# In-place quantization, seven tiles of x, and an order rule for chain matmuls in layer 0 of a two-layer transformer kernel

## The chip, the cores and the metric

The kernel runs on one core of one Trainium2 chip. The metric is the device time of one launch in microseconds (us), as the median of several executions. A core has five instruction queues that run side by side, each in its own order: TensorE (PE, matmuls, with the weight loads PEld beside them), VectorE (DVE), ScalarE (ACT), GpSimd (POOL) and SyncE (SP, which here only issues DMAs). An instruction that waits holds up everything behind it in its queue.

## What is computed

The input x is 16 sequences of 512 tokens, 128 wide. Two layers follow each other; the change touches only the first:

```
x = x + 0.5 * ffn0(layernorm(x))      # half-step feed-forward, I = 352
x = x + attn0(layernorm(x))           # 16 heads of 8, relative positions in a band of +-64
x = x + 0.5 * ffn0(layernorm(x))      # the same feed-forward again

def fp4_linear(x, w):                 # ffn0: gate, up and down are all of this form
    # both sides: blocks of 16 values, scale = max|x|/6, round to the grid 0 .5 1 1.5 2 3 4 6
    return einsum(quant(x), quant(w))
score = q.k + q.rel_emb_k[dist];  attn = softmax(score)
ctx   = attn.v + attn.rel_emb_v[dist]
```

Layer 1 (linear attention and a mixture of experts, each in half-steps) reads the result from DRAM. Its code is not changed.

## The kernel before, in words

Layer 0 is a software pipeline over 32 units: 16 sequences `b`, two halves `h` of 256 tokens each, unit `u = 2b+h`. A unit passes these steps, written as Python generators that yield after each small step:

- **head** and **tail** (`F.half`, L107 to L140): the first and the second feed-forward of a half. Layer norm (`ln_steps`, L48 to L63), quantization (`quant_steps`, L64 to L82), transposes of the quantized x (L115), gate and up matmuls (L121, L125) with the activation between (ACT L122, DVE L123, L126), quantization of `h`, transposes (L133), two ACT copies (L135, L136), down matmuls (L139), and the sum into x on DVE (L140). This is a chain: each link is a few tenths of a us on another engine. `quant_steps` runs on DVE (L70 to L78) and ends in two POOL instructions (L79, L81); it writes the scaled values into a tile `q_y` of its own.
- **prep**, **prepV**: the projections to q, k and v, written to DRAM as f16 pairs and read back in the layout of the scores (`BD`, `TQ`, `KS`).
- **maxima** (L333 to L356): all 32 score tiles of a unit are computed on PE (`scores`, L255 to L267: four matmuls L263, eight more L267 where the tile lies in the band), and DVE takes the maxima of each (L341, at high priority). Then DVE reduces them (`mk`, L347), PE transposes the result (L349), and the negative maximum goes by DRAM into a row of `BD`. I call these scores X.
- **main** (L358 to L415): the same 32 score tiles again, now with the maximum subtracted; ACT writes the exponentials (L369) into `PT`. I call these scores M. Both kinds take turns in one PSUM pool `sps` of three tiles. After every eight M scores a run of 16 matmuls averages v (`av`, L272 and L274); for the relative values there are band runs (`rps`) of 16 or 32 matmuls, copied by ACT (L403). At the end the band part goes through DRAM (`RD`, then `cr`).
- **fin** (L417 to L444): DVE adds the two parts (`cx`, L422), PE transposes (L430), DVE divides (L433, L434), PE transposes again (L437), ACT copies (L438), PE multiplies with the output weights (L440), and DVE adds into x (L443).

`interleave` (L446) sets the order in which these generators emit. Each has a number of steps and a start and an end in units; the generator whose next step is due first goes next. A main has 59 steps in its unit (32 scores, four empty steps after each average, and others), the stream of maxima 33 per unit, fin starts 1.45 units after its main started. Tiles of x come from a pool of five; `xload(b)` is called in the first step of head(b).

The emitted order is not the issued order. A list scheduler with a timeline of its own sorts the instructions of each engine by priority and by when it believes them ready, so a chain matmul may stand in PE's queue before a score that was emitted earlier. `tc.issue_after(i)` adds an edge that only fixes the issue order on i's engine; it waits for nothing. `run` (L270) already uses it to keep a run together.

Of the kernel before, what the change touches and what calls it, by code (L numbers as in the profile page):

```python
# [8 lines left out]
F32 = mybir.dt.float32  # L9
# [16 lines left out]
class K:  # L26
# [23 lines left out]
    def ln_steps(s, xb, out, wk, n):  # L50
# [12 lines left out]
        yield  # L63
    def quant_steps(s, X, wk, P, nb, tag):  # L64

# [7 lines left out]
        y=wk.tile([128,max(704,n)],F32,name=("q_y","q_yw")[n>704])[:,:n]; y3=y.rearrange("p (b k) -> p b k",k=16)  # L73
# [10 lines left out]
class FFN:  # L84
# [22 lines left out]
    def half(f, xb, half, wk, pp):  # L107
# [3 lines left out]
        xn=wk.tile([128,2,128],F32,name="f_x")  # L111
# [3 lines left out]
        for j in range(2): nc.tensor.transpose(ps[:,j*128:(j+1)*128],xq[:,j*128:(j+1)*128],s.ident)  # L115
        xqT=wk.tile([128,256],F32,name="f_x"); nc.scalar.copy(xqT,ps[:,:256]); yield
        h=wk.tile([128,2,I],F32,name="f_h")
        for j in range(2):
            t=h[:,j,:]
            g=pp.tile([128,512],F32,name="mps")  # L120
            nc.tensor.matmul(g[:,:I],xqT[:,j*128:(j+1)*128],f.wguT[:,0,:],start=True,stop=True)  # L121
            nc.scalar.activation(t,g[:,:I],AF.Tanh,scale=0.5)  # L122
            nc.vector.scalar_tensor_tensor(t,t,1.0,g[:,:I],ALU.add,ALU.mult); yield  # L123
            u=pp.tile([128,512],F32,name="mps")
            nc.tensor.matmul(u[:,:I],xqT[:,j*128:(j+1)*128],f.wguT[:,1,:],start=True,stop=True)  # L125
            nc.vector.scalar_tensor_tensor(t,u[:,:I],0.5,t,ALU.mult,ALU.mult); yield  # L126
        for hq in s.quant_steps(h.rearrange("p a b -> p (a b)"),wk,128,44,"hq"): yield
        hq=hq.rearrange("p (a b) -> p a b",a=2)
        for j in range(2):
            ps=pp.tile([128,512],F32,name="mps")  # L130
            for c in range(3):
                P=min(128,I-c*128)
                nc.tensor.transpose(ps[:P,c*128:(c+1)*128],hq[:,j,c*128:c*128+P],s.ident)  # L133
            hT=wk.tile([128,3,128],F32,name="hT",bufs=1)
            nc.scalar.copy(hT[:,0:2,:],ps[:,:256])  # L135
            nc.scalar.copy(hT[:96,2,:],ps[:96,256:384])  # L136
            for c in range(3):
                P=min(128,I-c*128)
                nc.tensor.matmul(ps[:,384:512],hT[:P,c,:],f.wdT[:P,c,:],start=(c==0),stop=(c==2),skip_group_check=True)  # L139
# [6 lines left out]
class Attn0:  # L146
# [110 lines left out]
    def scores(a, out, kt, half, b, BD, TQ, KS):  # L257
# [4 lines left out]
        for g in range(4):  # L262
            nc.tensor.matmul(o4[:,g],KS[:,sd,g*512+kt*128:g*512+(kt+1)*128],BD[:,g,:,b*32:b*32+32].rearrange("p h (x j) -> p x h j",j=4),start=(g==0),stop=(not ib and g==3),skip_group_check=True)  # L263
        if ib:
            for x in range(8):
                w0=kt*128-blk*32-x+a.OFF
                nc.tensor.matmul(out[:,x*64:x*64+64],a.ET[:,w0:w0+128],TQ[:,:,b*32+4*x:b*32+4*x+4],start=False,stop=(x==7),skip_group_check=True)  # L267

    xnT={}; pend={}; last=None
# [5 lines left out]
    def prep(a, b, xb, wk, pM):  # L275
# [6 lines left out]
        for j in range(4): nc.tensor.transpose(ps[:,j*128:(j+1)*128],xn[:,j,:],a.ident)  # L282
        xnT=a.xnT[b]=wk.tile([128,512],F32,name="xnT",bufs=2); nc.scalar.copy(xnT,ps); yield
        for z in range(2):
            ps=pM.tile([128,512],F32,name="mps")
            nc.tensor.matmul(ps,a.w[:,z*128:(z+1)*128],xnT,start=True,stop=True)
# [18 lines left out]
        nc.tensor.matmul(ps[:32],a.eb.rearrange("p a b -> p (a b)"),q,start=True,stop=True)  # L305
# [26 lines left out]
    def maxima(a, b, half, wk, pS, pM):  # L332
# [13 lines left out]
        for hh in range(2):  # L346
            nc.vector.tensor_reduce(mk[:,hh],mx.rearrange("p k (x s) b -> p s b x k",s=2)[:,hh],axis=AX.X,op=ALU.max)  # L347
        ps=pS.tile([128,512],F32,name="sps")
        nc.tensor.transpose(ps[:,:128],mk.rearrange("p s b x -> p (s b x)"),a.ident)  # L349
# [8 lines left out]
    def main(a, b, half, X, wk, big, pS, pA, pM):  # L358
        s=a.s; nc=a.nc; i=b%2
        u=(2*b+half)%3; BD=a.BD[u]; TQ=a.TQ[u]; KS=a.KS[b%2]; V=a.V[b%2]; RD=a.RD[half]; cr=a.cr[0]  # L360
        av=[pA.tile([128,512],F32,name=f"av{z}") for z in range(2)]
        RV=wk.tile([128,4,4,4,16],F32,name="RV")
        PT=[None]*4
        for kt in range(4):
            pt=big.tile([128,16,256],F32,name="PT"); PT[kt]=pt
            for bb in range(8):
                ps=pS.tile([128,512],F32,name="sps")
                a.scores(ps,kt,half,bb,BD,TQ,KS)
                nc.scalar.activation(pt[:,:,bb*32:bb*32+32].rearrange("p h (x j) -> p x h j",j=4),ps.rearrange("p (x h j) -> p x h j",x=8,j=4),AF.Exp)  # L369
                yield  # L370
            vs=a.vers(kt,half)
            mms=[]
            for z in range(4):
                for cg in range(4):
                    h=z*4+cg
                    o=av[z//2][cg*32:cg*32+32,(z%2)*256:(z%2)*256+256]
                    fs=(kt==0 and z%2==0)
                    mms.append(((o,V[:,2*kt-1+vs,h*9:h*9+32],pt[:,h,:]),dict(start=fs,stop=(kt==3),skip_group_check=True,tile_position=(0,cg*32))))
            a.run(mms)
            for _ in range(4): yield  # L380
            for hb in range(2):
# [3 lines left out]
                rps=pA.tile([128,512],F32,name="rps")  # L385
                first=[True]*4
                mms=[]
                for b0 in bl[::2]:
                    ok=[(bb,k) for k in reversed(ks) for bb in (b0+1,b0) if a.inband(k,half*8+bb)]
                    for n,(bb,k) in enumerate(ok):  # L390
                        blk=half*8+bb
                        for x in range(8):
                            cg=x%4; col=(bb-hb*4)*128+(x//4)*64
                            v0=(blk*32-k*128+a.UO)//8
                            mms.append(((rps[cg*32:cg*32+32,col:col+64],a.TV[a.vers(k,half)][:,x,v0-8*a.vers(k,half):v0-8*a.vers(k,half)+4,:].rearrange("p v d -> p (v d)"),
                                PT[k][:,:,bb*32+4*x:bb*32+4*x+4]),
# [641 lines left out]
```

## Time and profile before

| | us |
|---|---|
| time, median of 3 runs (3628.54 to 3629.66) | 3629.37 |
| the profiled execution's own time | 3633.94 |
| its span, first to last instruction | 3632.2 |
| PE busy | 2825.0 (78%) |
| DVE busy | 2444.9 (67%) |
| ACT busy | 1693.8 (47%) |
| POOL busy | 838.9 (23%) |

The busy time of an engine is the time in which at least one of its instructions ran. In the 40 slices of the page PE is busy at 8 to 9 tenths in the slices that lie between 270 and 1900 us; layer 0 ends near 2030 us. The transposes L349, one for each unit, start at 163.3 us for the first and 1923.8 us for the last; the stretch between them is 31 steady units, 56.8 us each, and is called the stage below. The granted clock is the share of TensorE's full clock that the chip's throttle allowed.

### The profile page before, as it was taken

The page shows a single profiled execution, that of the slowest core. Times are in us where ns is not written, and L with a number is a line of the kernel's source. Part 1 is how long each engine was busy: PE and PEld are TensorE (multiplying, and loading weights), DVE is VectorE, ACT ScalarE, POOL GpSimd, SP SyncE. Part 2 cuts the span into 40 slices and gives each one's busy share as a digit, 9 for nine tenths or more (in the row PEclk, how much of TensorE's full clock was granted, in tenths as well). Part 3 has the DMA queues.
Part 4 walks back from the last instruction along what each step waited for, and adds up shares of the span by engine and source line. Part 5 has one row for each costly group of instructions (what it writes and reads, how often), then busy time and mean ns, then how long its engine had stood idle before and what let it go on. Part 6 is the DMA issues. An engine that isn't in the chain of part 4 may idle for free. (4 is left out here: it accounts for less than half of the span.)

```text
span 3632.2 us, 95259 instructions
## 1 busy us (share of the span) xinstructions
PE 2825.0 (78%) x40077; PEld 2032.3 (56%) x40077; DVE 2444.9 (67%) x6508; ACT 1693.8 (47%) x3391; POOL 838.9 (23%) x789
## 2 busy tenths in 40 slices
PE   5578989889898889888896388873788888878570
PEld 3357777667676677666775244431565555555230
DVE  5568788777887788877773467774546655655356
ACT  3145555545455454545554155533455454445242
POOL 4122222222222222222110222212112211111226
PEclk8799999999999999999998599886899989989785
DMA  3232222321223222222210111104312222121401
GB/s 105 54 91 71 57 53 59 81 63 52 65 65 77 64 50 58 76 74 62 53 33 19 32 33 36 36 33 123 90 54 73 59 63 56 36 62 36 126 17 46
DMA packets 290159, 217.23 MB, mean 60 GB/s; under 512 B 77402, under 2 KB 257476, under 8 KB 289604
## 3 DMA queue, kind: packets, MB, share of 16 engines
q1 hardware_dynamic: 284468, 207.72, 21.6%
q8 instruction: 315, 5.16, 0.6%
q10 hardware_dynamic: 5264, 3.43, 0.4%
q14 instruction: 112, 0.92, 0.1%
HBM read 110.28 MB, written 100.78 MB: 58 GB/s over the span
## 5 line engine op out<-in xcount | busy, mean ns | idle before, releaser
L341 DVE TRANSPOSE_TENSOR_REDUCE mx<-sps 128x16 f32<-128x512 f32 x1024 | 702.5, 701 | 261.7 <-PE sps L263 137.2
L263 PE MATMUL sps<-a_BD,a_KS 128*128 128x128 f16 x8192 | 736.4, 222 | 136.2 <-DVE mx L341 65.6
L369 ACT ACTIVATE PT<-sps 128x512 f32<-128x512 f32 x1024 | 576.4, 599 | 433.8 <-PE sps L267 238.1
L263 PEld LDWEIGHTS <-a_KS 128*128 128x128 f16 x8192 | 546.1, 98 | 296.4 <-issue 260.0
L59 POOL TENSOR_TENSOR ln_rs<-ln_ve,negh 128x4 f32<-128x4 f32 (+1 forms) x192 | 176.9, 930 | 855.1 <-DVE ln_ve L58 760.6
L267 PE MATMUL sps<-a_TQ,a_ET 128*128 128x64 f16 x7168 | 370.3, 195 | 0.0
L721 DVE SCALAR_TENSOR_TENSOR moe<-mps,oh,moe 128x128 f32<-128x128 f32 x896 | 289.8, 341 | 110.7 <-PE mps L719 96.5
L79 POOL TENSOR_TENSOR q_M<-q_y,q_M 128x704 f32<-128x704 f32 (+2 forms) x129 | 157.0, 1218 | 784.6 <-DVE q_y L78 658.6
L719 PE MATMUL mps<-f_W,T 128*128 128x512 f32 x512 | 297.1, 701 | 24.8 <-DVE moe L721 20.0
L267 PEld LDWEIGHTS <-a_ET 128*128 128x128 f16 x7168 | 311.2, 99 | 2.3 <-issue 1.9
L274 PE MATMUL av<-PT,a_V 128*32 128x256 f32 x3840 | 251.9, 387 | 0.0
L894 DVE TENSOR_TENSOR a_at<-pp,a_cm 128x1024 f32<-128x1024 f32 x128 | 154.3, 1214 | 79.6 <-PE pp L892 78.6
L892 PE MATMUL pp<-a_F 64*128 64x128 f32 x2048 | 169.8, 306 | 41.4 <-DVE a_at L894 30.2
L892 PEld LDWEIGHTS pp<-a_F 64*128 64x128 f32 x2048 | 143.3, 206 | 93.0 <-DVE a_at L894 36.9
L719 PEld LDWEIGHTS mps<-f_W,T 128*128 128x128 f32 x512 | 102.7, 222 | 125.0 <-issue 75.3
L274 PEld LDWEIGHTS av<-PT,a_V 128*32 128x32 f32 x3840 | 121.4, 111 | 68.7 <-issue 5.0
L874 ACT ACTIVATE a_F<-pp 128x1024 f32<-128x1024 f32 x128 | 127.0, 1025 | 46.8 <-PE pp L872 40.5
L62 ACT ACTIVATE xn<-xn,ln_mr,ln_rs 128x128 f32<-128x128 f32 x256 | 103.6, 481 | 95.5 <-DVE ln_mr L60 75.2
L274 PE MATMUL rps<-PT,a_TV 128*32 128x64 f32 x6912 | 134.5, 222 | 4.6 <-issue 4.4
L139 PE MATMUL mps<-wdT,hT 128*128 128x128 f32 (+1 forms) x768 | 126.9, 301 | 5.6 <-ACT hT L136 4.0
L673 ACT COPY f_PT<-St 32x512 f32<-32x512 f32 x128 | 78.7, 615 | 106.0 <-DVE St L672 99.9
L872 PE MATMUL pp<-a_QK,a_PK 128*128 128x512 f16 x256 | 82.7, 413 | 54.4 <-DMA a_QK<-a1d 26.6
(342 smaller groups left out, 5330.2 us busy)
## 6 DMA issues: line engine op xcount, KB each, us to landing
QM<-a_HM SPq DMA_DIRECT2D x180, 128.0 KB
a_TQ<-QM SPq DMA_DIRECT2D x120, 192.0 KB
RD<-RV SPq DMA_DIRECT2D x32, 512.0 KB
a_KS<-KSd SPq DMA_DIRECT2D x128, 96.0 KB
a_QK<-a1d SPq DMA_DIRECT2D x128, 96.0 KB
xn<-X SPq DMA_DIRECT2D x32, 256.0 KB
a1d<-a_hi SPq DMA_DIRECT2D x64, 128.0 KB
a_BD<-QS SPq DMA_DIRECT2D x128, 58.0 KB
```

The lines of the kernel that those rows point to most:

```text
L59: nc.gpsimd.tensor_tensor(rs,ve,s.negh[:,:n],ALU.pow); yield
L79: nc.gpsimd.tensor_tensor(M[:P],y[:P],M[:P],ALU.subtract)
L263: nc.tensor.matmul(o4[:,g],KS[:,sd,g*512+kt*128:g*512+(kt+1)*128],BD[:,g,:,b*32:b*32+32].rearrange("p h (x j) -> p x h j",j=4),start=(g==0 ...
L267: nc.tensor.matmul(out[:,x*64:x*64+64],a.ET[:,w0:w0+128],TQ[:,:,b*32+4*x:b*32+4*x+4],start=False,stop=(x==7),skip_group_check=True)
L274: for p,q in mms[1:]: a.nc.tensor.matmul(*p,**q)
L341: with a.s.tc.high_priority(): r=nc.vector.tensor_reduce(mx[:,kt,:,bb],ps.rearrange("p (i c) -> p i c",c=32),axis=AX.X,op=ALU.max,apply_tr ...
L369: nc.scalar.activation(pt[:,:,bb*32:bb*32+32].rearrange("p h (x j) -> p x h j",j=4),ps.rearrange("p (x h j) -> p x h j",x=8,j=4),AF.Exp)
L719: nc.tensor.matmul(ps,yT[:,j*128:(j+1)*128],a.W[:,e2*4:e2*4+4,:],start=True,stop=True)
L721: nc.vector.scalar_tensor_tensor(moe[:,j,:],ps[:,e*128:(e+1)*128],oh[:,j,e2*4+e:e2*4+e+1],moe[:,j,:],ALU.mult,ALU.add)
L874: nc.scalar.activation(f,ps,AF.Relu)
L892: nc.tensor.matmul(ps[:,hh,bs],f[hh*64:hh*64+64,1,bs],f[hh*64:hh*64+64,0,bs],start=True,stop=True)
L894: nc.vector.tensor_tensor(k,ps.rearrange("p h (b q) -> p (h b) q",b=4),a.cm.unsqueeze(1).to_broadcast([128,8,128]),ALU.mult)
```

## The change

Five edits, all in layer 0:

1. `quant_steps` no longer has the tile `q_y`: it works in place (`y=X`). The tiles `f_x` get three buffers instead of two.
2. x has seven tiles instead of five, four are loaded at the start, and `xload` is a generator of its own, due 1.25 units before the first step of head(b).
3. main's steps are its 32 scores and nothing else. Average runs, band runs, their copies and the end (the DMAs to `RD` and `cr`, the copies to `cx`) go into a list `todo`; after each score one entry is taken from it. What is left after the last unit is emitted by `rest`.
4. `scores` records its last matmul in `lastmm`, and `gate()` puts every chain matmul of head, tail, prep, fin and the transpose L349 behind the score emitted last (`issue_after`).
5. Steps: a yield is added before the transpose L349, between the copies and the down matmuls, and between L438 and L440; the step counts follow; fin starts at 1.6 units instead of 1.45.

```
-        y=wk.tile([128,max(704,n)],F32,name=("q_y","q_yw")[n>704])[:,:n]; y3=...
+        y=X; y3=X3
...
+    def gate(s):
+        return s.tc.issue_after(s.lastmm) if s.lastmm is not None else ExitStack()
...
-        xn=wk.tile([128,2,128],F32,name="f_x")
+        xn=wk.tile([128,2,128],F32,name="f_x",bufs=3)
...
-            nc.tensor.matmul(g[:,:I],xqT[:,j*128:(j+1)*128],f.wguT[:,0,:],start=True,stop=True)
+            with s.gate(): nc.tensor.matmul(g[:,:I],xqT[:,j*128:(j+1)*128],f.wguT[:,0,:],start=True,stop=True)
...
             hT=wk.tile([128,3,128],F32,name="hT",bufs=1)
             nc.scalar.copy(hT[:,0:2,:],ps[:,:256])
-            nc.scalar.copy(hT[:96,2,:],ps[:96,256:384])
+            nc.scalar.copy(hT[:96,2,:],ps[:96,256:384]); yield
...
+        a.s.lastmm=getattr(r,"ins",r)          # at the end of scores()
...
             nc.vector.tensor_reduce(mk[:,hh],...)
+        yield
         ps=pS.tile([128,512],F32,name="sps")
-        nc.tensor.transpose(ps[:,:128],mk.rearrange("p s b x -> p (s b x)"),a.ident)
+        with a.s.gate(): nc.tensor.transpose(ps[:,:128],mk.rearrange("p s b x -> p (s b x)"),a.ident)
...
                 nc.scalar.activation(pt[...],ps...,AF.Exp)
+                if a.todo: a.todo.pop(0)()
                 yield
...
-            a.run(mms)
-            for _ in range(4): yield
+            a.todo.append(lambda kt=kt: avrun(kt))
...
+                a.todo+=[lambda hb=hb,b0=b0,ks=ks: rvrun(hb,b0,ks) for b0 in bl[::2]]+[lambda hb=hb: rvcopy(hb)]
+            if kt==3: a.todo.append(end)
+    def rest(a):
+        while a.todo: a.todo.pop(0)(); yield
...
-        ct=wk.tile([128,2,128],F32,name="cn")...; nc.scalar.copy(ct,ps[:,:256])
+        ct=wk.tile([128,2,128],F32,name="cn")...; nc.scalar.copy(ct,ps[:,:256]); yield
...
-        xk=c.enter_context(tc.tile_pool(name="xk",bufs=5))
+        xk=c.enter_context(tc.tile_pool(name="xk",bufs=7))
...
-            if b<nb: xload(b); yield from F.half(X[b],h,fk,pF)
+            if b<nb: yield from F.half(X[b],h,fk,pF)
...
-        W=dict(part=0,V=(.6,.7),fin=(.45,.9),prep=(0,.7),tail=1.0,head=(-.1,1))
+        W=dict(part=0,V=(.6,.7),fin=(.6,1.0),prep=(0,.7),tail=1.0,head=(-.1,1))
...
-        S=[(part(99999),33*2*nb,W['part'],2*nb+W['part'])]
+        S=[(part(99999),34*2*nb,W['part'],2*nb+W['part'])]
...
-                at(A.main(b,h,X,wk,big,pS,pA,pM),59,0,1)
+                at(A.main(b,h,X,wk,big,pS,pA,pM),32,0,1)
...
+                if h==1 and b+hl+1<nb: at(xl(b+hl+1),1,-.35,-.3)
...
+        S.append((A.rest(),8,2*nb,2*nb+.15))
```

## The prediction

> **What bounds the kernel now.** I read the time by stage first, then PE's rows in the steady stage, then the waits, then single stalls in the timeline. By windows (columns: stretch, length, busy us and count of PE, PEld, DVE, ACT, POOL, then granted clock, DMA share, GB/s):
>
> ```profile
> 163.40:1923.80 1760.40, 1551.47 (x27900) 1225.71 (x27901) 1369.79 (x3018) 884.81 (x1938) 395.34 (x369) 0.97 0.25 62
> 1923.80:2030.00 106.20, 60.72 (x902) 43.66 (x902) 38.48 (x113) 39.48 (x90) 17.31 (x24) 0.76 0.07 18
> 2030.00:3632.20 1602.20, 1129.35 (x10729) 704.62 (x10728) 944.82 (x3133) 732.43 (x1286) 370.85 (x338) 0.84 0.20 57
> ```
>
> In the stage PE is busy 88.1%, DVE 77.8%: PE sets the pace, 208.9 us of it are idle, and DVE stands close behind. Layer 1, the third row, keeps its program; in the built order 96% of its PE instructions keep their place. It counts as unchanged. PE's groups in the stage, with the idle time before each:
>
> ```profile
> L263 PE MATMUL sps<-a_BD,a_KS 128*128 128x128 f16 x7888 | 705.3, 222 | 110.5 <-DVE mx L341 60.1 <-ACT PT L369 34.4 <-issue 2.9
> ...
> L430 PE MATMUL mps<-ident,cx 128*128 128x128 f32 x240 | 38.6, 286 | 8.9 <-DVE f_h L126 6.1 <-DVE cx L422 2.6
> ...
> L440 PE MATMUL mps<-a_wo,cn 128*128 128x128 f32 x116 | 21.2, 306 | 13.5 <-ACT cn L438 11.4 <-issue 2.1
> ...
> L437 PE MATMUL mps<-ident,cn 128*128 128x128 f32 x59 | 18.3, 310 | 22.0 <-DVE a_V L321 19.8 <-DVE qklo L307 2.2
> ...
> L349 PE MATMUL sps<-ident,mk 128*128 128x128 f32 x31 | 9.7, 314 | 21.5 <-DVE mk L347 10.7 <-DVE hq_sc L71 9.9 <-DVE ln_mv L56 0.9
> ```
>
> So 57.0 us lie before three chain matmuls, L349, L437 and L440, and 110.5 before scores that wait for one of the three `sps` tiles. One source of the latter shows in DVE's waits, as seen at one place in the timeline:
>
> ```profile
> DVE ln_st L55 <- DMA x<-in_L_attn_x_dram: 45.5, 11, 5.2
> ```
>
> ```profile
> 412.11 0.40 SPq L475 DMA_DIRECT2D x<-in_L_attn_x_dram  x1
> ...
> 415.46 1.06 DVE L55 BATCH_NORM_STATS2 ln_st<-x 128x6 f32<-128x128 f32 x5 [4.33 <-DMA x<-in_L_attn_x_dram]
> ...
> 418.07 0.58 PE L263 MATMUL sps<-a_BD,a_KS 128*128 128x128 f16 x4 [3.07 <-DVE mx L341]
> ```
>
> The load of x is issued just before its layer norm; DVE waits 4.33 us in order, the maxima behind it wait, the score tiles stay full, PE idles 3.07 us. It happens 11 times. The third cost is the clock (windows again):
>
> ```profile
> 416.80:423.60 6.80, 5.53 (x68) 5.46 (x68) 6.31 (x24) 3.55 (x10) 1.36 (x2) 0.50 0.28 72
> ...
> 816.10:819.50 3.40, 2.95 (x27) 2.86 (x27) 2.86 (x7) 2.02 (x5) 0.87 (x1) 0.50 0.49 120
> ...
> 351.00:411.00 60.00, 55.61 (x969) 45.47 (x973) 50.10 (x108) 32.45 (x72) 16.26 (x14) 1.00 0.12 30
> ```
>
> The clock falls to 0.50 for 3.4 us or a multiple. Stepping through the stage I find 23 such windows, 95 us together: ten (40.9 us) right after an x stall, six (20.5 us) right after a wait before L440, as at 816.1, where L440 had idled 1.82 us. The last row is the best stretch: PE 92.7% busy, full clock.
>
> **A: three chain links.** In the built order of both programs I counted what PE has between a matmul and the one that needs its result through another engine. From L437 to L440: two scores before, eight to ten and usually a run after. From the last score of the maxima to L349: one score and a run, or two scores; after, two or three scores and a run. From the first L430 to the first L437: mostly two scores and a run; after, four to eight scores. The links cost 0.39 us (ACT L438), 1.1 (two of L347 at 554 ns) and 0.5 (L433 223 ns, L434 271 ns), plus the queue of ACT or DVE; a score costs 0.24 us outside the band (three in 0.85 us, less the last one's drain) and 0.46 in it, a run of averages 1.87. The work now covers the links: 57.0 us of idle, of which I leave 7. **-50** (bounds -57 to -25, if half comes back as buffer waits).
>
> **B: the x stalls.** With seven tiles the load follows the store that frees its tile, and stands over a unit (56.8 us) ahead of its use; landing took 4 us. On SP it moves past one unit's loads of `KS`, `BD` and `TQ`; it waits there for the store's landing, but so it did before, and these loads too are issued a unit ahead. PE's idle time inside the 11 stalls and 1.5 us after sums to 19.4. **-19** (bounds -19 to -10).
>
> **C: the clock.** 61.4 us of half-clock windows follow A or B. Work in them takes twice as long, so at most 30.7 us come back; part of each window waits for DVE anyway. **-22** (bounds -31 to 0). The Trainium skill ("TensorE: Matmul & The Clock Gate", section "HAM oscillation — how this bites in real kernels") says to avoid PE idle gaps over about 3.4 us. It speaks against this term, since most waits here are shorter; by it alone, of the waits in A and B, only the 3.89 us gap at 762 would count and C would be an estimated -3. The trace has a window at 0.50 after a wait of 1.82 us, so I keep the row.
>
> **D: the transposes L430.** The two additions L422 (1.12 us each) now stand on DVE beside quantization steps, and L430 waits for a tile that DVE frees after them. For each PE wait I took the PE work between it and the matmul that feeds its producer, and subtracted the producer's duration and 0.2 us; the shortfalls at L430 sum to 13 us before (8.9 measured) and 34 after. **+10** (bounds -9 to +21).
>
> **E: score tiles.** By the same count the shortfalls of scores are 104 us before (91 measured, without B) and 158 after. Against this: of 1994 neighbouring scores 863 were of one kind before, 171 after. Two X in a row cost DVE 0.70 us each where PE needs 0.24 or 0.46, and that queue is not in my count; and in strict turns three neighbours' shortfalls share one stall, which the count takes three times. Neither sign is excluded; DVE, 44.2 us of work per unit, rises from 77.8% to some 81%. **+8** (bounds -30 to +54).
>
> **F: the end of layer 0**, the second row: L430 of unit 30 idles 9.87 us for `cr`; it now has 17 scores and two runs of averages between the last band run and itself instead of 13 and one, while the list's rest comes at the very end. **-3** (bounds -10 to +10).
>
> **Edits at nothing.** In-place quantization: the same instructions on the same sizes; a tile of `h` is held from L74 to L79, 567+498+852+1692 ns = 3.6 us longer, hidden because two tiles serve two streams that each use one for less than half a unit; uncovered, 3.6 us a half. Empty steps, yields and `issue_after` edges issue nothing. Averages move by a score or two; `PT` has three buffers.
>
> Sum: -50-19-22+10+8-3 = -76. The profiled execution took 3633.94, its span 3632.2 and 1.74 around it; it lies 4.57 above the median. 3633.94-76 = 3557.9, less 4.57: **3553 us**, -2.1%; a unit falls from 56.8 to about 54.5 us.
>
> **Rivals.** *Slower: the ring of score tiles.* Strict turns tie every M score to DVE: X frees the tile that M takes. If the shortfalls come out in full (E +54, D +21), the stalls keep the clock falling (C 0), and half of A returns (-25), then -25-19+54+21-3 = +28: 3657. It decides once the idle time before L263 passes about 150 us with the windows at 0.50 still there. For it: DVE's work is 91% of PE's (1369.79 over about 1504 at full clock) and three tiles are a short queue. Against: 351 to 411 has the same ratio (90%) and 92.7%.
>
> *Less: the waits move.* What L349, L437 and L440 no longer wait for, the scores wait for; only B and the cost of its windows (40.9/2, less a quarter) remain: -19-15 = -34, 3595. For it: 94.5 us of L263's idle already comes from DVE and ACT.
>
> *More: the whole stage runs as 351 to 411.* PE's 1551.5 us less 47 for the slow windows, at 92.7%: 1623, so -137: 3492. For it: that stretch ends where the first x stall begins, and has a full clock. Against: DVE is in order, with steps up to 2.2 us (two L422).
>
> **Chances.** Forecast 0.43, less 0.22, more 0.22, slower 0.13. The first alone spans 3520 to 3590. The range 3480 to 3640 takes in the other three up to most of the last. About 0.2% (7 us) is what a measurement can tell from no change: faster has the first, the third and most of the second, 0.85; same 0.04 from the edges of second and last; slower 0.11.
>
> **What would show it.** Right: L349, L437 and L440 together idle under 10 us, no wait of L55 on x, ten or fewer windows at 0.50 in the stage, L263's idle 80 to 110 us, L349's 31 periods near 54.5 us. Wrong: L263's idle over 150 us, the clock still 0.97 in the stage, L430 idle over 35 us, or layer 1 more than 5 us off its 1602.

## The result, and the profile after

The changed kernel takes 3738.61 us (median of 4 runs, 3735.62 to 3749.23) against 3629.51 us for the kernel before beside it: ratio 1.0293, interval 1.0263 to 1.0324. It is slower by 2.9%, and the time lies outside the forecast range. The profiled execution took 3735.62 us, its span is 3733.9 us, 101.7 us longer than before.

Windows of the changed kernel, cut at the first and the last L359 (the transpose that was L349) and at the end of layer 0; the columns are those of the windows in the prediction:

```profile
0.00:152.10 152.10, 71.12 (x504) 49.78 (x504) 75.37 (x203) 31.70 (x61) 45.51 (x50) 0.79 0.38 96
152.10:2044.50 1892.40, 1589.52 (x27925) 1257.66 (x27926) 1391.72 (x3049) 914.16 (x1950) 401.12 (x375) 0.93 0.22 58
2044.50:2145.00 100.50, 62.99 (x925) 46.27 (x922) 47.79 (x131) 41.86 (x94) 21.00 (x26) 0.79 0.08 19
2145.00:3733.90 1588.90, 1123.60 (x10728) 699.67 (x10728) 939.05 (x3126) 732.32 (x1286) 370.65 (x338) 0.85 0.20 58
```

The stage grew by 132.0 us (61.0 us a unit instead of 56.8); the start (163.4 before), the end and layer 1 became shorter by 11.3, 5.7 and 13.3. Of the 132, PE's idle time is 94 (208.9 to 302.9) and its busy time 38: the same matmuls, but the granted clock fell from 0.97 to 0.93. Stepping through the stage I find 259.4 us at 0.50, where there were 95.6. PE's groups in the stage follow, with the idle time before each and what ended it. The changed kernel numbers its lines anew: the scores L263 are now L269, the gate matmul L121 is L126, the split into `qkhi` and `qklo` L307 is L316, and L430, L437, L440 and L349 are L445, L453, L457 and L359.

```profile
L269 PE MATMUL sps<-a_BD,a_KS 128*128 128x128 f16 x7880 | 727.5, 223 | 168.0 <-DVE mx L350 90.5 <-ACT PT L417 53.4 <-DMA a_BD<-QS 13.4
L126 PE MATMUL mps<-wguT,f_x 128*128 128x352 f32 x234 | 106.3, 539 | 101.3 <-ACT f_x L121 99.9 <-DVE f_h L131 0.6 <-DVE qklo L316 0.6
...
L445 PE MATMUL mps<-ident,cx 128*128 128x128 f32 x232 | 37.3, 284 | 14.3 <-DVE qklo L316 7.7 <-DVE f_h L131 6.0 <-DVE cx L436 0.6
...
L453 PE MATMUL mps<-ident,cn 128*128 128x128 f32 x58 | 17.9, 325 | 1.2 <-DVE cn L449 0.3
L457 PE MATMUL mps<-a_wo,cn 128*128 128x128 f32 x116 | 17.7, 275 | 0.0
...
L359 PE MATMUL sps<-ident,mk 128*128 128x128 f32 x31 | 9.0, 290 | 0.4 <-DVE mk L356 0.4
```

The three links (L359, L453, L457) are quiet: 1.6 us together instead of 57.0. The wait of DVE for x is gone. But a line that had no part in the prediction, the gate matmul L126 (L121 before, 6.0 us), now idles 101.3 us, waiting for ACT's copy L121, and the scores L269 idle 168.0 instead of 110.5. ACT's waits in the stage (us in total, times, longest) say why L121 was late. First after, then the row of before that the prediction did not read:

```profile
ACT RV L401 <- DMA RD<-RV: 134.9, 14, 12.2
```

```profile
ACT RV L403 <- DMA RD<-RV: 21.1, 9, 4.0
```

ACT cannot copy the band part into the tile `RV` before the DMA of the last unit has read it; there is one such tile. The timeline shows one of these waits: SP, then ACT, then PE (start, length, engine, line; in brackets the idle time and its releaser).

```profile
454.01 3.43 SPq L339 DMA_DIRECT2D a_TQ<-QM  x1
457.55 0.69 SPq L504 DMA_DIRECT2D X<-x  x1
462.61 0.39 SPq L491 DMA_DIRECT2D x<-in_L_attn_x_dram  x1
463.09 0.55 SPq L404 DMA_DIRECT2D RD<-RV  x1
```

```profile
448.60 1.03 ACT L401 COPY RV<-rps 128x128 f32<-128x128 f32 x4
...
473.20 1.01 ACT L401 COPY RV<-rps 128x128 f32<-128x128 f32 x4 [11.31 <-DMA RD<-RV]
474.02 0.41 ACT L121 COPY f_x<-mps 128x256 f32<-128x256 f32 x1
```

```profile
474.48 1.54 PE L126 MATMUL mps<-wguT,f_x 128*128 128x352 f32 x2 [9.54 <-ACT f_x L121]
```

Read it from the end. PE waited 9.54 us for L121, which stood in ACT's queue behind the copies L401; these waited 11.31 us for `RD<-RV`. The data for that DMA was ready at 449.6, but SP issued it at 463.09: first came the loads of `KS`, `BD` and `TQ` (until 457.44), the store of x, and the load of the next x, which itself waited for that store to land (4.4 us). From issue to the next copy 10.1 us pass. The same place before, SP and ACT:

```profile
408.83 0.39 SPq L486 DMA_DIRECT2D X<-x  x1
412.11 0.40 SPq L475 DMA_DIRECT2D x<-in_L_attn_x_dram  x1
...
430.46 0.72 SPq L406 DMA_DIRECT2D RD<-RV  x1
```

```profile
419.09 1.03 ACT L403 COPY RV<-rps 128x128 f32<-128x128 f32 x4
...
440.13 1.05 ACT L403 COPY RV<-rps 128x128 f32<-128x128 f32 x4 [1.65 <-DMA RD<-RV]
```

Before, `RD<-RV` was issued 10.3 us after its copies, landed within another 9.7, and the next copies waited 1.65 us: the chain was already without slack. A stall also has a price in clock (windows of after; length, then busy times, then the granted clock):

```profile
467.50:477.70 10.20, 3.22 (x8) 1.68 (x9) 2.06 (x6) 3.32 (x10) 0.00 (x0) 0.50 0.16 48
```

The clock falls inside the stall and stays at 0.50 for 3.2 us after it ends.

In the middle of the stage the stalls come once in two units, at the second half of a sequence: the intervals of L359 alternate between about 53 and 71 us there, where those of L349 stood between 56 and 59 before. Not all of this difference is the stall: in rd_on_act below, where it is gone, they still alternate between about 54 and 63.

### The profile page after: what moved, and what is told of

The parts are those of the page before. It is cut to its first block, busy times and chain, and to the rows that moved or that the text cites. A ratio compares the mean times of both kernels' runs of the same rounds, so it can differ in the third digit from the quotient of the medians.

```text
span 3733.9 us, 95130 instructions
## 1 busy us (share of the span) xinstructions
PE 2847.2 (76%) x40077; PEld 2053.4 (55%) x40077; DVE 2453.9 (66%) x6508; ACT 1720.0 (46%) x3391; POOL 838.3 (22%) x789
## 5 line engine op out<-in xcount | busy, mean ns | idle before, releaser
L269 PE MATMUL sps<-a_BD,a_KS 128*128 128x128 f16 x8192 | 759.1, 223 | 208.5 <-DVE mx L350 92.6
L417 ACT ACTIVATE PT<-sps 128x512 f32<-128x512 f32 x1024 | 600.4, 598 | 550.2 <-PE sps L269 276.0
L269 PEld LDWEIGHTS <-a_KS 128*128 128x128 f16 x8192 | 569.2, 99 | 384.8 <-issue 340.3
L83 POOL TENSOR_TENSOR q_M<-f_h,q_M 128x704 f32<-128x704 f32 x64 | 108.1, 1690 | 707.5 <-DVE f_h L82 597.7
L914 DVE TENSOR_TENSOR a_at<-pp,a_cm 128x1024 f32<-128x1024 f32 x128 | 154.2, 1214 | 73.6 <-PE pp L912 72.7
L126 PE MATMUL mps<-wguT,f_x 128*128 128x352 f32 x256 | 116.8, 541 | 102.2 <-ACT f_x L121 100.8
L401 ACT COPY RV<-rps 128x128 f32<-128x128 f32 x256 | 67.0, 414 | 198.9 <-DMA RD<-RV 134.9
```

Of the source, the lines that this page charges most:

```text
L269: r=nc.tensor.matmul(o4[:,g],KS[:,sd,g*512+kt*128:g*512+(kt+1)*128],BD[:,g,:,b*32:b*32+32].rearrange("p h (x j) -> p x h j",j=4),start=(g= ...
L914: nc.vector.tensor_tensor(k,ps.rearrange("p h (b q) -> p (h b) q",b=4),a.cm.unsqueeze(1).to_broadcast([128,8,128]),ALU.mult)
```

## The experiments

All ratios are against runs of the kernel before on the same chip. Theory 1, formed from the trace: the late `RD<-RV` on SP is the cause. Rival: strict turns leave the scores without tiles (the slower rival of the prediction).

### Is it the late DMA of the end?

```diff
-            nc.sync.dma_start(RD[...],T["RV"])        # rd_on_act
+            nc.scalar.dma_start(RD[...],T["RV"])
```

> The changed kernel, with one edit: the DMA that writes the band tile RV to DRAM is issued from ScalarE's queue instead of SyncE's. Theory 1 (RV wait): there is one RV tile; in the changed kernel its DMA stands on SyncE behind a unit's loads and behind the load of x, so it lands 22 us after the copies that filled RV; the next unit's copies wait for it on ScalarE (134.9 us in 14 waits), the copy of the transposed x waits behind them, and the gate matmul holds TensorE (99.9 us in the stage). Issued by ScalarE right after its own copies, the DMA is done in about 10 us and the wait goes: ScalarE's wait on RD under 20 us, the gate matmul's under 10, the two kinds of unit both near 53 us, time 3540 to 3620. Theory 2 (ring of score tiles): strict turns of the two kinds of scores bind TensorE to VectorE; the wait before L269 (168 us in the stage) stays, and the time stays above 3690. Theory 3 (the order rule puts chain matmuls in the wrong place): the gate matmul waits as long for something else, time above 3690.

Measured: 1.003 (1.0008 to 1.0052). The stalls are gone, as theory 1 says, but the median is 3653.6 us where it expected 3540 to 3620: the scores still idle 182.0 us, as theory 2 says, and 177.5 us of the stage run at 0.50. PE's groups in its stage:

```profile
L269 PE MATMUL sps<-a_BD,a_KS 128*128 128x128 f16 x7880 | 731.7, 225 | 182.0 <-ACT PT L417 88.6 <-DVE mx L350 69.8 <-DMA a_BD<-QS 13.1
...
L126 PE MATMUL mps<-wguT,f_x 128*128 128x352 f32 x234 | 97.9, 500 | 2.6 <-ACT f_x L121 1.1 <-DVE qklo L316 0.7 <-DVE f_h L131 0.6
```

One word in one line takes back 2.6%, about half of what lies between the forecast (0.979 of before) and the result. The Trainium skill ("Trainium Kernel Development and Optimization", section "Key Constraints") says that issuing DMAs from several engines "only saves the sequencer's issue time". Here it saved more, the place in the queue: `RD<-RV` was issued 3.1 us after its copies instead of 13.2.

Two tiles instead of one take the wait away too, if there is room for them:

```diff
-            if hb==0: T["RV"]=wk.tile([...],F32,name="RV")            # both
+            if hb==0: T["RV"]=wk.tile([...],F32,name="RV",bufs=2)
-        xk=...(name="xk",bufs=7)
+        xk=...(name="xk",bufs=5)     # rv_two_x_five
+        xk=...(name="xk",bufs=6)     # rv_two_x_six; f_x with 2 buffers, rc in mt's tile
```

> The changed kernel with two RV tiles; the room is paid with five tiles of x instead of seven, the early load of x kept. Theory 1 (RV wait): the copies no longer wait for the DMA of the unit before, though that DMA is as late as before; ScalarE's wait on RD under 10 us, no 9 us stall of the gate matmul, time 3540 to 3620. Theory 2 (ring of score tiles): still above 3690. If this one falls and the kernel with the DMA on ScalarE does not, the wait matters and the lateness does not; if it is the other way round, the late DMA costs through the part that it feeds (the additions before L445).

Measured: 1.0396 (1.0357 to 1.0435). A miss: the x stalls came back larger (DVE waits 174.9 us for x, in 11 stalls), so this run can't judge the second tile.

> The changed kernel with two RV tiles; the room is paid with six tiles of x instead of seven, two f_x tiles instead of three, and the small tile rc sharing mt's place. Unlike the run with five tiles of x, whose load of x waited on SyncE for its tile (174.9 us of VectorE's time), six should be enough for the early load. RV wait: the copies find a free tile, ScalarE's wait on RD is under 10 us, ratio to before between 0.98 and 1.01, as with the DMA on ScalarE (1.003). If the late DMA itself costs (through the additions before L445), above 1.01. If the tile was not the cause, 1.02 or more.

Measured: 1.0108 (1.0079 to 1.0137). No wait of ACT on `RD`, no stall at L126; 172.7 us before the scores and 30.0 before L445, of which 27.4 wait for DVE's split L316, which itself waits 73.9 us for the DMAs that empty `qkhi` and `qklo`. So a second way of removing the wait removes the stall, too.

Bringing the end forward, with turns and rule as they are:

```diff
-                if a.todo: a.todo.pop(0)()        # two_entries
+                for _ in range(2):
+                    if a.todo: a.todo.pop(0)()
```

> The changed kernel with two entries of the list taken after each score instead of one: turns and rule as they are, but runs and the end are emitted sooner. RD<-RV should be issued under 9 us after its copies instead of 13.2, or the next unit's copies stand further behind; the row of L401 waiting on RD falls below 60 us (134.9), the time to 1.000 to 1.012. If the row stays above 100 us, the length of the list is not what makes the end late, and the time stays at 1.025 to 1.035.

Measured: 1.0269 (1.0235 to 1.0303); ACT's wait is 138.5 us, and `RD<-RV` is still issued 13.5 us after its copies. The length of the list is not what makes the end late.

And the place of the load of x:

```diff
-            if b<nb: yield from F.half(X[b],h,fk,pF)              # old_load_step
+            if b<nb: xload(b); yield from F.half(X[b],h,fk,pF)
-        xk=...(name="xk",bufs=7)
+        xk=...(name="xk",bufs=5)
```

> The changed kernel with the x part of edit 2 undone: five tiles of x, loaded again in the first step of head(b). All else, the order rule and the score steps among it, stays. If the wait of the copies of the band part (L401) on the load RD<-RV needs the load of x and its wait for the store standing ahead of it in SP's queue, then the row of L401 on RD falls from 134.9 to under 40 us, the stalls of 9 us before the up matmuls go, and the time comes to 1.000 to 1.010 of the kernel before (the x stalls, some 20 to 30 us with their clock, are back). If the place of the end in the order is enough with the rule, the row stays above 100 us and the time is 1.030 or more.

Measured: 1.0477 (1.0454 to 1.0499). ACT's row did fall, to 20.4 us, but for another reason than the one expected: SP's order stayed the same (loads, store, load of x, `RD<-RV` 13.5 us after its copies), but the next copies came 29.2 us after the last instead of 23.4, because now the load of x was the late one, whose user waits on DVE:

```profile
464.88 0.87 DVE L55 BATCH_NORM_STATS2 ln_st<-x 128x6 f32<-128x128 f32 x4 [15.34 <-DMA x<-in_L_attn_x_dram]
```

So the block on SP is there with the early load and without it. What early loading adds is that x no longer suffers from it.

### Which edit brings it?

```diff
-                at(A.main(b,h,X,wk,big,pS,pA,pM),32,0,1)    # old_main: the changed kernel with the
+                at(A.main(b,h,X,wk,big,pS,pA,pM),59,0,1)    # old body of main and no list (edit 3 undone)
...
-                at(A.main(b,h,X,wk,big,pS,pA,pM),59,0,1)    # before_portions: the kernel before with
+                at(A.main(b,h,X,wk,big,pS,pA,pM),32,0,1)    # the new body and the list (edit 3 alone)
...
-            nc.sync.dma_start(RD[...],T["RV"])              # before_portions_rd_act: on top of that
+            nc.scalar.dma_start(RD[...],T["RV"])
...
-            if b<nb: xload(b); yield from F.half(X[b],h,fk,pF)   # before_early_x: the kernel before
+            if b<nb: yield from F.half(X[b],h,fk,pF)             # with edits 1 and 2 alone
+                if h==1 and b+hl+1<nb: at(xl(b+hl+1),1,-.35,-.3)
```

> The changed kernel with edit 3 undone: main emits its average and band runs, copies and its end itself, in 59 steps, as before; in place, seven x tiles, the order rule and the steps of the others as changed. Theory 1 (RV wait): the end's DMA is emitted before the next unit's loads again, so the 9 us stalls go and the gains that I forecast for the chain links and the x stalls show: 3540 to 3600. Theory 2 (ring, from the strict turns of scores, which edit 3 makes): the turns go too, so this falls as well, to about 3560 to 3630, and only the comparison with the two RV kernels tells which. Theory 3 (order rule): stays above 3690.

Measured: 0.992 (0.9889 to 0.9951), faster than both kernels. ACT waits 8.7 us for `RD`, the scores idle 110.6. Edit 3 is thus worth 3.7% of loss in the changed kernel.

> The kernel before with edit 3 alone: average and band runs, copies and the end as list entries, one after each score; five x tiles, late x load, no order rule. Theory 1 (RV wait comes from edit 3 alone, since it moves the end's DMA behind the next unit's loads): ScalarE waits over 80 us on RD and the ratio to before is 1.015 to 1.04. Theory 2 (it takes the order rule to turn the wait into a stall, since without the rule TensorE goes round the chain matmul): the wait on ScalarE is there but the ratio is below 1.015.

Measured: 1.0119 (1.0091 to 1.0147), with ACT waiting only 9.1 us for `RD`. Theory 1 in its simple form (edit 3 makes the stall) falls: alone it doesn't. What it does cost lies at the transposes of `cx`, which idle 72.3 us (8.9 before), 54.7 of them for the split into `qklo`; the half clock rose to 228.7 us.

> The kernel before with edit 3 and the RV tile's DMA issued by ScalarE. What is left of edit 3 is its strict turns of the two kinds of scores. Ring of score tiles: TensorE's idle time before scores rises from 6.2 us per two units to about 10 and the ratio is 1.00 to 1.02. My forecast's reading (turns are neutral or help): the idle time stays at 6.2 or falls, ratio 0.98 to 1.00.

Measured: 1.0026 (1.0008 to 1.0043). The scores idle 112.2 us, as before: edit 3 alone doesn't drain the tiles either.

> The kernel before with edits 1 and 2 alone: quantization in place, three f_x tiles, seven tiles of x and the early load. My step B and its share of C: the eleven waits of VectorE on x go (45.5 us of VectorE), 19 us of TensorE's idle time and some 15 us of half clock with them: 3629 - 34 = 3595, between 3585 and 3615. Rival: the early load delays something else on SyncE (it waits there for a store), and the time stays at 3629 or rises; then the DMA of RV shows later on SyncE than 5.7 us after its copies.

Measured: 0.9949 (0.9929 to 0.9969), about half of the gain expected, though inside its range. Its PE groups show why (the numbering is that of the kernel before):

```profile
L430 PE MATMUL mps<-ident,cx 128*128 128x128 f32 x240 | 42.7, 308 | 62.0 <-DVE qklo L307 52.5 <-DVE cx L422 9.0 <-DVE f_h L126 0.5
...
L437 PE MATMUL mps<-ident,cn 128*128 128x128 f32 x59 | 20.5, 348 | 2.7 <-DVE qklo L307 2.1 <-DVE a_V L321 0.6
...
L440 PE MATMUL mps<-a_wo,cn 128*128 128x128 f32 x116 | 19.6, 290 | 1.3 <-issue 1.1 <-ACT cn L438 0.2
...
L349 PE MATMUL sps<-ident,mk 128*128 128x128 f32 x31 | 10.7, 347 | 6.8 <-DVE mk L347 6.3 <-DVE ln_mv L56 0.5
```

Two things stand here. The three links idle 10.8 us instead of 57.0, though no rule touches them: most of that idle time goes with edits 1 and 2, of which the early load is the likely one (no run has them apart). And 52.5 us have moved to L430, behind DVE's split L307, which waits 50.8 us for the DMA that empties the single tile `qklo` (7.7 before).

The band part's distances tell how the edits meet. From the timelines, medians of ten units of the second halves (fifteen in the three rows that name the edits 4 or 5), counted from the end of the copies of the band part:

| kernel | `RD<-RV` issued after (us) | next copies start after (us) | ACT's wait on `RD` in the stage (us) |
|---|---|---|---|
| before | 9.9 | 19.8 | 21.1 |
| before_portions (edit 3) | 4.3 | 16.2 | 9.1 |
| before_early_x (edits 1, 2) | 12.7 | 23.0 | 12.5 |
| changed kernel | 13.2 | 23.4 | 134.9 |
| old_main (edits 1, 2, 4, 5) | 10.8 | 21.0 | 8.7 |
| no_rule (edits 1, 2, 3, 5; see below) | 9.1 | 19.3 | 31.0 |
| old_load_step (edits 1, 3, 4, 5) | 13.5 | 29.2 | 20.4 |
| rd_on_act | 3.1 | 17.0 | none listed |
| rv_two_x_six (two tiles) | 12.9 | 13.2 | none listed |
| old_main_rd_act (see below) | 1.2 | 21.1 | none listed |

The next copies can't start sooner than about 10 us after the issue. Where nothing holds them they follow after 21 us in the old main (last row) and after 13 to 17 us with edit 3 (the two rows above it); an issue after 4.3 us then costs little (second row). Edits 1 and 2 put the issue at 12.7 us, which the old main just bears (third row). In the changed kernel it is 13.2+10 = 23 us where 13 to 17 would do. This sum is the stall; no single edit shows it.

Which edits the late issue needs beside edit 3 is not settled: no run has edits 1 to 3 alone with one `RV` and `RD<-RV` on SP. In three units each, read from the timelines, what stands on SP between the copies and `RD<-RV` differs. In before_early_x it is 11 to 12 us of loads and the load of x, which takes under 1 us. In the changed kernel it is about 8 us of loads, then the store of x and the 5 us until it has landed and the load of x follows. The same stands there without the early load (old_load_step). Without the rule (no_rule) no store stands there, the issue comes after 9.1 us, and ACT's wait on `RD` falls to 31.0 us in ten. This points at the rule of edit 4, but DVE's long waits in that run (see below) may move the copies and the store as well, so it is not shown.

Then the rule of edit 4, off in both mains:

```diff
-        return s.tc.issue_after(s.lastmm) if s.lastmm is not None else ExitStack()
+        return ExitStack()        # old_main_no_rule (edit 3 undone), no_rule (edit 3 kept)
```

> The changed kernel with edit 3 undone (0.992 of before) and the order rule off as well; the yields and step counts of edit 5 stay. Chain links: if the rule makes the gain at L349, the transposes of cn and L440's matmuls, their idle time comes back (57 us) and the ratio rises to 1.00 to 1.015. If the yields alone do it, the idle time stays under 25 us and the ratio stays within 0.005 of 0.992. If the rule does harm (it fixes places that go stale), the ratio falls below 0.987.

Measured: 1.0098 (1.0063 to 1.0134): with the steps of edit 5 the rule is worth 1.8%, and against before_early_x (0.9949) edit 5 alone costs 1.5%. Of the links only L359 idles again, about 35 us; L445's counterpart idles 34.9 and the scores 151.9 (110.6 with the rule).

> The changed kernel without the order rule of edit 4: issue_after is not applied to the chain matmuls, all else stays. Theory: the score idle beyond the old 91 to 100 us needs the rule and the strict turns together, so the idle before the scores falls from 168 to about 100 us; the idle before the three chain links comes back with 40 to 60 us; whether the late DMA of the end still stalls the up matmuls is what the run shows. With it 1.02 to 1.03, without it 1.00 to 1.015. Rival: the strict turns alone with the early x load raise the score idle; then it stays above 150 us.

Measured: 1.0508 (1.0482 to 1.0533). The time is beyond both sides. The scores idle 262.6 us, above the rival's 150, but DVE's split now waits 127.1 us for the DMA of `qklo` and 72.7 for that of `qkhi`. With late DMAs in the way the score idle says nothing on turns. Of the three links 26.9 us came back, all before L359.

### With a second `qklo`, and `RD<-RV` on ACT

The single tile `qklo` had shown up in most of these runs. It gets a second buffer, and x six tiles instead of seven.

```diff
-            ...lo=wk.tile([128,512],F16,name="qklo")           # all but old_main_rd_act
+            ...lo=wk.tile([128,512],F16,name="qklo",bufs=2)
-        xk=...(name="xk",bufs=7)     # old_main_two_qk: on old_main; early_x_two_qk: on before_early_x
+        xk=...(name="xk",bufs=6)
...
-        nc.sync.dma_start(RD[...],RV)       # old_main_rd_act: on old_main, alone
+        nc.scalar.dma_start(RD[...],RV)
```

> The changed kernel with edit 3 undone (main with its old 59 steps) and the DMA RD<-RV issued by ACT instead of SP. In old_main the copies of the band part hardly waited for RD, so if the price of the late DMA belongs to the list of edit 3, this gains nothing: 0.988 to 0.995 of the kernel before, as old_main with 0.992. If part of it was left in old_main too (SP holding RD<-RV behind loads), 0.980 to 0.986.

Measured: 1.0121 (1.0093 to 1.0149), a miss on both sides: 59.7 us are now idle before L449 (there the transposes of `cn`), behind DVE's split, which waits 25.3 us for the DMA `KSd<-qklo` (10.8 in old_main). That RD's move shifted the other DMAs is likely, not shown. Another queue is no gain by itself.

> The changed kernel with edit 3 undone, six tiles of x instead of seven, and two tiles qklo instead of one (the room of one x tile). In old_main DVE's split into qkhi and qklo (L316) waits for the DMA that empties the single qklo, and the chain matmuls behind it stall some 20 us. If these stalls are a cost of their own, the idle before the matmuls that wait for qklo falls from about 20 us to under 5 and the time comes to 0.980 to 0.987; if the wait only moves to the score tiles, it stays at 0.990 to 0.994. The sixth x tile in place of the seventh is expected to cost nothing, as a load still stands half a sequence ahead; if x waits appear (L55 on x above 20 us), that has to be taken off.

Measured: 0.9868 (0.9839 to 0.9896). L453, L449 and L359 (there the three links) idle 7.0 us together, 75.1 us run at half clock (95.6 before), 108.0 are idle before the scores.

> The kernel before with edits 1 and 2 (in place, early load of x, here with six tiles) and two tiles qklo; main and chain order as before. In before_early_x DVE's wait for the single qklo cost L430 52.5 us, which hid half of what the x stalls gave back. With it gone the terms B and C should show: 0.980 to 0.988, under 90 us of half clock. If the wait moves to the scores: 0.990 to 0.995.

Measured: 0.9834 (0.9802 to 0.9866), the best run, though its interval overlaps that of old_main_two_qk. Its stage, from the first to the last L349:

```profile
169.10:1869.60 1700.50, 1536.65 (x27900) 1214.87 (x27901) 1361.32 (x3018) 890.98 (x1940) 385.38 (x369) 0.98 0.26 64
```

That is 54.9 us a unit. It has quantization in place, early x and one more small buffer, no rule, no added steps, the old main.

The last four were to show what edits 3, 4 and 5 do when the late DMAs are out of the way (`RD<-RV` on ACT, two `qklo`). In three of them they were not, as the rows below the results show.

```diff
-            nc.sync.dma_start(RD[...],T["RV"])    # all four, on the changed kernel, with two qklo and six x
+            nc.scalar.dma_start(RD[...],T["RV"])
...
-        return s.tc.issue_after(s.lastmm) if s.lastmm is not None else ExitStack()
+        return ExitStack()              # rd_act_two_qk_no_rule, no_steps_no_rule: edit 4 off
...
-        W=dict(...fin=(.6,1.0)...)      # no_steps_rule, no_steps_no_rule: edit 5 undone,
+        W=dict(...fin=(.45,.9)...)      # the yields and the step counts too
```

> The changed kernel with RD<-RV issued by ACT, two tiles qklo and six tiles of x. No DMA that SP issues late is left to hold ACT or DVE. Theory: strict turns with the rule leave the scores short of tiles by themselves; then the idle before the scores stays at 145 to 170 us, and the time at 0.993 to 1.003 of the kernel before, against 0.987 with the old main. Rival: the score idle was the late qklo (21 us of waits of L316 and what follows them); then it falls under 120 us and the time comes to 0.978 to 0.988.

Measured: 0.9985 (0.9966 to 1.0004), the theory's time, with the scores idle for 188.6 us, above its range.

> As rd_act_two_qk, and the order rule of edit 4 not applied. If the rule makes the score idle together with the turns, that falls to about 100 us, the links before L359, L445 and L457 idle 40 to 60 us, and the time is about the same, 0.995 to 1.005. If the turns do it alone, the score idle stays above 145 us, the links come on top, and the time is 1.010 to 1.025.

Measured: 1.0206 (1.0166 to 1.0247), as the second expectation has it, but with late DMAs of `qklo` in the way (below).

> As rd_act_two_qk (all late DMAs off the path), with edit 5 undone: no added yields, the step counts of before, fin starts at 1.45 units. If the strict turns make the score idle, it stays at 145 to 190 us and the time at 0.993 to 1.005 of the kernel before. If it is the later fin and the added steps that crowd DVE at one place, the score idle falls under 120 us and the time comes to 0.978 to 0.990.

Measured: 0.9993 (0.9978 to 1.0009). The score idle fell as the second expectation has it, the time did not.

> The kernel before with edits 1, 2 and 3, two tiles qklo and RD<-RV on ACT: edits 4 and 5 undone. Against early_x_two_qk (0.983) it differs in the main alone and in the queue of RD. If strict turns cost by themselves, 1.000 to 1.020 and the score idle above 140 us; if edit 3 costs only with edits 4 or 5, 0.980 to 0.992 and about 80 to 100 us.

Measured: 0.9937 (0.9915 to 0.9958), just above the second expectation, as is the score idle of 103.2 us.

The scores' row of rd_act_two_qk, then that of no_steps_rule with the row that took over:

```profile
L269 PE MATMUL sps<-a_BD,a_KS 128*128 128x128 f16 x7880 | 721.5, 224 | 188.6 <-ACT PT L417 109.9 <-DVE mx L350 58.1 <-DMA a_BD<-QS 11.4
```

```profile
L269 PE MATMUL sps<-a_BD,a_KS 128*128 128x128 f16 x7880 | 716.5, 220 | 128.2 <-DVE mx L350 52.6 <-ACT PT L416 40.9 <-DMA a_BD<-QS 11.7
...
L295 PE MATMUL mps<-xnT,a_w 128*128 128x512 f32 x60 | 41.9, 789 | 49.1 <-DVE f_h L128 48.1 <-ACT xnT L292 1.1
```

DVE's longest waits for a DMA in the stage of no_steps_rule, no_steps_no_rule and rd_act_two_qk_no_rule (rd_act_two_qk has single waits only, of 11.6 us and less):

```profile
DVE cx L435 <- DMA a_cr<-RD: 52.8, 14, 5.3
```

```profile
DVE qkhi L316 <- DMA QS<-qkhi: 98.1, 15, 13.4
```

```profile
DVE qklo L316 <- DMA QS<-qklo: 94.3, 13, 8.5
```

In no_steps_rule fin starts earlier, and DVE waits in it for `cr`, the band part by way of DRAM; twelve of the thirteen long waits of L295 end 2.6 us after such a wait. Most of what the scores gained went there.

| edits, all with two `qklo` | score idle in the stage (us) | DVE's waits for the DMAs of `qkhi`, `qklo` and `cr` (us) | ratio |
|---|---|---|---|
| 1, 2 | 90.2 | 27.2 | 0.983 |
| 1, 2, 4, 5 | 108.0 | 19.5 | 0.987 |
| 1, 2, 3 | 103.2 | 114.7 | 0.994 |
| 1, 2, 3, 4 | 128.2 | 66.9 | 0.999 |
| 1, 2, 3, 4, 5 | 188.6 | 20.4 | 0.999 |
| 1, 2, 3, 5 | 197.3 | 130.5 | 1.021 |

The great shortfall of score tiles comes where the turns of edit 3 and the steps of edit 5 are together. With the rule this is clean of late DMAs (188.6 against 108.0, with 20.4 and 19.5 us of DVE's waits); without it (197.3) they are in the way. Edit 3 costs 1.2% with edits 4 and 5 (RD's queue differs as well) and 1.0% without them, there with 114.7 us of DVE's waits for DMAs in the price. The rule repairs what edit 5 breaks (1.021 to 0.999); where edit 5 is absent the kernel with it is 0.6% slower, and its late `cr` may be the reason.

## Why the prediction was wrong, point by point

In the forecast's terms the profiled span moved so: L126, which the sum didn't have, +95 us; the scores' idle time (B and E) +57.5; the three links (A) -55; L430 (D) +5; PE's busy time in the stage (C) +38; the end (F) -6, the start -11, layer 1 -13; PE's other waits make up the rest to +101.7.

**A, three links, -50.** The sign to look for came: 57.0 to 1.6 us. But the gain was not A's. With edits 1 and 2 alone, the same three lines idle 10.8 and, with a second `qklo`, 12.5 us (9.1, 1.2 and 2.2). Some 45 of the 57 us go with edits 1 and 2 (21.7 of them come back at L430, which idles 30.6 in that kernel), and the rule has little left to earn: 0.983 without edits 4 and 5, 0.987 with them, intervals overlapping. I counted A and B as separate because they were different rows. DVE being late from x is the likely link, since L437's idle time ended with a DVE instruction of another step (`a_V`, 19.8 us); no run isolates it.

**B, x stalls, -19.** The wait is gone. The failed step is here: "On SP it moves past one unit's loads ... it waits there for the store's landing, but so it did before". I asked what the load of x would wait for, not who stands behind it on SP. Before, the load waited at 412.11 and `RD<-RV` was issued 18 us later; in the changed kernel `RD<-RV` stands right behind the load, and its wait of 4.4 us is part of the 13.2. That the early load alone put it there is not shown: old_load_step has the same order. The term was also too small: 19.4 us counts PE's idle time until 1.5 us after each wait of DVE, but the eleven waits of L263 that follow end 2.6 us after it and come to 31.6.

**"Edits at nothing": "Averages move by a score or two".** This is the other half of the failed step. I checked `PT` (three buffers) and not `RV` (one), nor the DMA that empties it. The row that warned was in the trace of before: ACT's wait on `RD`, nine times, 4.0 us at most. A wait that ends late nine times out of 31 has no slack to give, and edit 3 took 4 to 8 us of the distance. Priced: L126 idles 101.3 us, and removing the wait gives 1.0293 to 1.003, or 2.6%. That is nearly all of the loss against before, but half of the miss: 1.003 is still 2.4% above the forecast's 0.979. In that kernel the scores idle 182.0 us and 177.5 us run at half clock, so what is left shows in E and C.

The same part says that yields and empty steps "issue nothing". They issue nothing, but they place everything after them: edit 5 without the rule is where the worst rows are (1.021, and 1.0098 with the old main).

**C, the clock, -22.** Wrong in the changed kernel: 95.6 to 259.4 us at 0.50, and PE's busy time rose by 38 us. Nine stalls of 9.2 to 10.4 us each brought its window, 95.6 us together, of which 55.8 lie inside the stalls. The term has the right sign only in early_x_two_qk (68.3 us) and old_main_two_qk (75.1), at most 14 us of work; with the x waits gone and one `qklo` the half clock rose even so, to 113.9 in before_early_x and 143.4 in old_main. The -3 beside it counted one wait; three of the x stalls' waits are above 3.4 us (3.89, 3.61 and 3.48, the last two at 1460.94 and 1116.27), so by that count it would have been an estimated -7, half of their windows of 6.8, 3.4 and 3.4 us.

**D, L430, +10.** 8.9 to 14.3 us, +5.4: within its bounds.

**E, score tiles, +8 (-30 to +54).** The term starts from the 91 us that are left without B, so 168.0 us are +77, well beyond the upper bound; without the RV stalls 182.0, or +91. I chose a middle value between two signs and had the row for the upper end: the count of shortfalls, 104 to 158. The gain I set against it, fewer neighbours of one kind, shows in no run.

**F, the end of layer 0, -3.** -5.7, within its bounds. Layer 1, called unchanged, is 13.3 us shorter in the one profiled execution of each kernel; why is open.

**The rivals.** The slower one named an idle time over 150 us before the scores with the windows at 0.50 still there, and both came. But it was not the cause of most of the loss against before: with the RV stall gone and the score idle at 182 us, the time is 1.003, where the rival's 3657 would be 1.008. No case held a DMA that became late on SP.

**What stays open.** Why edits 3 and 5 together drain the score tiles; which of edits 1, 2, 4 and 5 make `RD<-RV` late beside edit 3; and by which route edits 1 and 2 quiet the links.

## What to carry to other kernels

When a step moves, list the DMAs on each side of it in their queue, and for each the tile that it frees and how many of that tile there are: a single buffer emptied by a DMA on a crowded queue is a chain as hard as any arithmetic. Look for short waits that occur often (here 21.1 us in nine): they mark chains without slack, and edits that each take a few us can add up to a stall. Two idle rows with one common source are one gain, so remove the source first and read the rows again before pricing the second edit. And when a run is to have a wait out of the way, read its waits before drawing on it: here another late DMA had taken the place in three runs of four.

## What the runs showed of the hardware

In the stalls of 9 us the granted clock fell during the stall: of the 10.2 us at 0.50 around the stall that ends at 474.48, 7.0 lie inside it, so a stall of 9.5 us cost only 3.2 us of slow work on top. With short waits the window came after them, and in proportion to the idle time these are dearer: behind two waits of L269 close together, 1.8 and 1.2 us, the changed kernel had a window of 3.4 us at 0.50 (at 631.3, and again at 1252.6), in which PE was busy 3.3 us. In the 3.4 us ahead of the first of them PE had been busy 1.07 us.
